# One PSUM pool for a whole network: rings turned by hand in place of a pool opened anew

## The chip, the cores and the metric

The kernel runs on one core of a Trainium2 chip. Its time is device microseconds (us) of one execution, from three executions of the kernel before: 2588.32, 2590.48 and 2588.38 us, median 2588.38 us. A fourth execution was profiled; it took 2587.3 us. A core has five engines[...]: TensorE (PE, matmuls), VectorE (DVE), ScalarE (ACT), GpSimd (POOL) and SyncE (SP, which issues DMAs here). TensorE writes its results into PSUM, eight banks of 128 x 512 float32 values; VectorE and ScalarE read them there.

## The reference

A small network of four residual layers on an input of 4 images, each 512 channels by 32 x 32 positions, so T = 1024 tokens. Each layer normalizes its input by groups of channels and adds its result to it.

```python
x = x + L0(gn(x))   # attention, 8 heads: scores mixed across heads, softmax,
                    # instance norm of the whole map, values, projection
x = x + L1(gn(x))   # channel gate: means -> 9-qubit circuit -> linear -> sigmoid
x = x + L2(gn(x))   # plain attention, 8 heads of 64: q, k, v, softmax, values, projection
x = x + L3(gn(x))   # memory: scores against 2048 items, top 8, softmax, weighted sum of 8 rows
```

Layers 2 and 3 are the ones that the change touches, with the end of layer 0. In layer 2 each head computes `softmax(q^T k / 8) v` over 1024 x 1024 scores; in layer 3 each token takes the 8 best of 2048 rows:

```python
q, k, v = conv(x, Wq), conv(x, Wk), conv(x, Wv)
out = conv(einsum(softmax(einsum(q, k) * SCALE), v), Wp)           # layer 2
att = tokens @ mempool.T                                             # layer 3
vals, idx = top_k(att, 8); out = softmax(vals) weighted rows mempool[idx]
```

## The kernel before

All arithmetic is float32. The program is one long list of instructions, traced by `fast_net` image by image; a second version, `general_net`, stands behind a branch that the inputs here never take. A scheduler orders the instructions of each engine; those wrapped in `pin(...)` keep the order in which they were written. The scheduler also places the semaphore waits: an instruction that overwrites a buffer waits for its last readers.

PSUM is used in two ways. For layer 0, a pool `ps_a` is opened at the top and gives out five fixed buffers: three pairs of banks, `pairs[0..2]` (each 128 x 2 x 512), and two single banks, `pv_bank` and `pt_bank`. The code names them itself: `project(..., at, ...)` takes `pairs[at % 3]` through `place` (L176). At L1434 to L1439 this pool is closed and two pools are opened in the same memory for layers 2 and 3: `ps_s` with three slots of two banks (tag `sc`) and `ps_m` with two slots of one bank (tag `mm`). From there a tile is asked for by `ps_s.tile(...)`, and the pool decides which slot it gets: the one that came free first in the order in which the scheduler placed the instructions.

The work around the change, in order of time:

- **End of layer 0, last image** (L1383 to L1432). The last steps of the attention run together with `take_q2`, the q projection of layer 2 for image 0 (`qs`, L1404). Then follow four k projections `ks[m](m + 1)` (L1413), the instance norm of the last image, four v projections `take_v2(0, i, i + 2)` (L1430, matmuls in L204), and four output projections `put_out(b, m, m)` (L1432, matmuls in L745). Each fills one pair of banks. q is taken out of PSUM by VectorE (L989), k by ScalarE (L996), v by VectorE (L1005). `put_out` ends in two VectorE additions per pair (L684), each followed by statistics (L699).
- **Layer 2** (L1458 to L1494). `UNITS2` cuts an image for one image into 16 units: 4 pairs of heads x 2 halves of the queries x 2 groups of four key blocks. `scores2` (L1009) computes four score tiles for a unit (L1027, two matmuls each into one pair of banks), and ScalarE takes their exponentials (L1021) into one of six places in SBUF. `apply2` (L1050) multiplies the exponentials of the unit before with v (L1064, eight matmuls into one `mm` bank). Of the four exponentials of a unit, two are issued before `apply2` and two inside it, after its first and second key block, because their place in SBUF is read by those matmuls. At every second unit `invert2` (L1084) sums the softmax denominators with two small matmuls (L1095) into an `sc` slot, which ScalarE copies out (L1099). POOL and VectorE add up exponentials for these sums (L1041, L1045, L1046, L1080, L1081). Small matmuls of the gate and the norms (`small_ps`, L1441) also take an `sc` slot for a moment.
- **Between images** the q, k and v projections of the next image and the output projection of this one run back to back (`place(None, ...)`, a slot of `ps_s`).
- **Layer 3** (L1515 to L1543): `attention` (L1170) fills two `sc` tiles per block of 128 tokens, `pick` finds the top 8 and gathers their rows, `read` and `read_last` transpose or sum the result through a `mm` bank (L1234, L1254).

Of the kernel before, what the change touches and what calls it, by code (L numbers as in the profile page):

```python
# [10 lines left out]
F32 = mybir.dt.float32  # L11
# [3 lines left out]
PSUM = bass.MemoryType.PSUM  # L15

P = 128
B = 4
C = 512
T = 1024  # L20
KC = C // P
TC = T // P
NB = 512
# [18 lines left out]
def fast_net(ctx: ExitStack, tc: tile.TileContext, a: dict, out: bass.AP, flag: bass.AP):  # L42
# [6 lines left out]
    stage = ctx.enter_context(ExitStack())  # L49
# [125 lines left out]

    def place(at, name):  # L176

        return pairs[at % 3] if at is not None else ps_s.tile([P, 2, NB], F32, tag="sc", name=name)

    def flat2(ps):  # L180
        return ps.rearrange("p n q -> p (n q)")
# [827 lines left out]
    def scores2(b, u, before=None):  # L1009

        m, n, t0 = u
        I = img[b]
        nm = f"c{b}_{m}_{n}"
        es, scs = [], []

        def exp2():
            e = places2[:, count[0] % 6]
            count[0] += 1  # L1020
            pin(nc.scalar.activation(e, scs[len(es)], AF.Exp))  # L1021
            es.append(e)

        for i, t in enumerate(range(t0, t0 + 4)):
            sc = ps_s.tile([P, 2, NB], F32, tag="sc", name=f"sc_{nm}_{t}")
            for r in range(2):
                pin(nc.tensor.matmul(  # L1027
                    sc[:, r, :],
                    I["k"][r * HD:(r + 1) * HD, m, t * P:(t + 1) * P],
                    I["q"][r * HD:(r + 1) * HD, m, n * NB:(n + 1) * NB],  # L1030
                    start=True, stop=True,
                ))
            scs.append(sc)
            if before is None or i < 2:
                exp2()
        if before is not None:
            apply2(b, before, exp2)
        I["e", u] = list(es)
        if t0 == 0:
            I["es", m, n] = sums2[:, (2 * m + n) % 2]  # L1040
            nc.gpsimd.tensor_add(I["es", m, n], es[0], es[1])  # L1041
            es = es[2:]
        for i in range(0, len(es), 2):
            two = pair_sum[:, (t0 + i) // 2 % 2]
            nc.gpsimd.tensor_add(two, es[i], es[i + 1])  # L1045
            nc.vector.tensor_add(I["es", m, n], I["es", m, n], two)  # L1046
        if t0 == TC - 4:
            over_keys(b, m, n)

    def apply2(b, u, exp2=None):  # L1050

        m, n, t0 = u
        I = img[b]
        if t0 == 0:
            invert2(b)
            I["pv", m, n] = ps_m.tile([P, NB], F32, tag="mm", name=f"pv_c{b}_{m}_{n}")
        else:
            finish2(b)
        pv = I["pv", m, n]
        for i, e in enumerate(I.pop(("e", u))):  # L1060
            t = t0 + i
            for r in range(2):
                h = 2 * m + r
                pin(nc.tensor.matmul(  # L1064
                    pv[r * HD:(r + 1) * HD, :], I["v"][:, t, h * HD:(h + 1) * HD],
                    e[:, r, :], start=(t == 0), stop=(t == TC - 1),
                ))
            if exp2 and i < 2:
                exp2()
        if t0 == TC - 4:  # L1070
            I["due"] = (m, n)
# [12 lines left out]
    def invert2(b):  # L1084

        I = img[b]
        due = I.pop("due", None)
        if due is None:
            return
        m, n = I["ready"] = due  # L1090
        nm = f"{b}_{m}_{n}"
        ps = ps_s.tile([P, 2, NB], F32, tag="sc", name=f"rs_{nm}")[:, 0, 0:NS]
        s_ = I.pop(("s", m, n)).rearrange("p r q -> p (r q)")
        for half in range(2):
            pin(nc.tensor.matmul(  # L1095
                ps[half * HD:(half + 1) * HD], same[:, half * HD:(half + 1) * HD], s_,
                start=True, stop=True))
        ri = small.tile([P, NS], F32, tag="ri", name=f"ri_c{nm}")
        nc.scalar.copy(ri, ps)  # L1099
        nc.vector.reciprocal(ri, ri)  # L1100
        ris = small.tile([P, NS], F32, tag="ssq", name=f"ris_{nm}")
        nc.vector.transpose(ris, ri)
        for bound, op in ((R_LO, ALU.is_ge), (R_HI, ALU.is_le)):
            nc.vector.scalar_tensor_tensor(seen0, ri, bound, seen0, op, ALU.add)
        rows = r_rows[n % 2]
        nc.sync.dma_start(out=rows, in_=ris[0:NS])
        rb = I["rb", m, n] = apool.tile([P, NB], F32, tag="rb", bufs=2, name=f"rb_c{nm}")
        for r in range(2):
            nc.sync.dma_start(
                out=rb[r * HD:(r + 1) * HD],  # L1110
                in_=rows.rearrange("(r q) x -> r (q x)", r=2)[r].partition_broadcast(HD))
# [58 lines left out]
    def attention(b, tt, between=None):  # L1170

        nm = f"{b}_{tt}"
        att = eight_k([P, NI], f"att_{nm}")
        for i, (lo, hi) in enumerate(
                ((0, T), (T, T + NB), (T + NB, NI)) if (b, tt) == tiles[-1] else ((0, T), (T, NI))):
            sc = ps_s.tile([P, T], F32, tag="sc", name=f"at_{nm}_{i}")
            for i0 in range(lo, hi, NB):
                for k in range(KC):
                    pin(nc.tensor.matmul(  # L1179
                        sc[:, i0 - lo:i0 - lo + NB],  # L1180
                        xn3[b][:, k, tt * P:(tt + 1) * P], memT[k][:, i0:i0 + NB],
                        start=(k == 0), stop=(k == KC - 1),
                    ))
            pin(nc.scalar.copy(att[:, lo:hi], sc[:, 0:hi - lo]))  # L1184
            if between is not None and i == 0:
                between()
        return att
# [43 lines left out]
    def read_last(b, tt, picked, dg):  # L1231

        got, et, rs, xr = picked
        tp = ps_m.tile([P, KC, P], F32, tag="mm", name=f"stp_{b}_{tt}")  # L1234
        for i in range(TOPK):
            for m in range(KC):
                pin(nc.tensor.matmul(
                    tp[:, m, :], got[:, i, m * P:(m + 1) * P], dg[:, i, :],
                    start=(i == 0 and m == 0), stop=(i == TOPK - 1),
                    skip_group_check=True,  # L1240
                ))
        return tp, xr

    def read(b, tt, picked):
        got, et, rs, xr = picked
        nm = f"{b}_{tt}"
        weigh(et, rs, nm)
        acc = apool.tile([P, NB], F32, tag="rb", bufs=2, name=f"acc_{nm}")
        pin(nc.vector.tensor_scalar_mul(acc, got[:, 0, :], et[:, 0:1]))
        for i in range(1, TOPK):  # L1250
            pin(nc.vector.scalar_tensor_tensor(  # L1251
                acc, got[:, i, :], et[:, i:i + 1], acc, ALU.mult, ALU.add
            ))
        tp = ps_m.tile([P, KC, P], F32, tag="mm", name=f"stp_{nm}")  # L1254
        for m in range(KC):
            pin(nc.tensor.transpose(tp[:, m, :], acc[:, m * P:(m + 1) * P], ident))
        return tp, xr
# [126 lines left out]
    for b in range(B):  # L1384
# [25 lines left out]
            collect_last(b)  # L1410
        load, take = statistics(b + 2) if b + 2 < B else (None, None)
        for m in range(KC):
            ks[m](m + 1)  # L1413
            next(state["behind"], None)
            for at in range(2 * m, 2 * m + 2):
                if load and m > 0:
                    take(at - 2)
                if load:
                    load(at)
# [3 lines left out]
        if last:  # L1423
            run_out(instance_norm(b))
            for n in range(KC):
                norm_quarter(b, n)
            bv2 = apool.tile([P, C], F32, tag="o2", name="bv2")
            nc.sync.dma_start(out=bv2, in_=a["bv"].partition_broadcast(P))
            for i in range(TC // 2):
                take_v2(0, i, i + 2)  # L1430
            for m in range(KC):
                put_out(b, m, m)  # L1432

    stage.close()  # L1434
    pairs.clear()
    by_scalar.append(True)
    stage = ctx.enter_context(ExitStack())
    ps_s = stage.enter_context(tc.tile_pool(name="ps_s2", bufs=3, space=PSUM))
    ps_m = stage.enter_context(tc.tile_pool(name="ps_m2", bufs=2, space=PSUM))  # L1439

    def small_ps(name):  # L1441
        return ps_s.tile([P, 2 * NB], F32, tag="sc", name=name)

    places2 = eT_flat[:, 0:6 * 2 * NB].rearrange("p (i r q) -> p i r q", i=6, r=2)
    sums2 = eT_flat[:, 6 * 2 * NB:8 * 2 * NB].rearrange("p (i r q) -> p i r q", i=2, r=2)
# [50 lines left out]
    def check_range():  # L1496

        tot = small.tile([P, 1], F32, tag="tot", name="tot")
        nc.vector.tensor_reduce(tot, seen0, AX.X, ALU.add)
        tps = ps_m.tile([P, NB], F32, tag="mm", name="tot")  # L1500
        nc.tensor.matmul(tps[:, 0:1], ones, tot, start=True, stop=True)
        nc.vector.tensor_scalar(
            flag, tps[0:1, 0:1], float(2 * P * NS * B * (TC + 2 * KC)), None, ALU.not_equal)
# [745 lines left out]
```

## Time and profile before

| | before |
|---|---|
| median of three runs | 2588.38 us (2588.32 to 2590.48) |
| profiled execution | 2587.3 us, span 2585.5 us |
| PE busy | 2533.4 us (98%), idle 47.3 us inside the span |
| ACT, DVE, POOL busy | 986.9, 1548.0, 1199.9 us |
| layer 0 | 0 to 1268.5 us |
| layer 2 | 1270.8 to 2123.1 us |
| granted TensorE clock | 0.999 of full speed |

The span runs from the first to the last instruction; 1.8 us of the profiled execution's time lie outside of it. PE is the engine to watch: it is busy nearly everywhere, so time can be won only where it idles, and is lost where it begins to wait. In the lines shown below, a timeline row has the start in us, the duration, the engine, the line of the program, the operation with what it writes and reads, and in square brackets how long the engine had stood idle before it and what ended that. A row of the waits has the waiter, what it waited for, the total in us, how often, and the longest.

### The profile page before, as it was taken

How to read it: one execution, taken by the hardware profiler on the slowest of the kernel's cores; microseconds unless marked ns; L12 is line 12 of the kernel's file. 1: busy time of each engine (PE TensorE's matmuls, PEld its weight loads, DVE VectorE, ACT ScalarE, POOL GpSimd, SP SyncE). 2: the span in 40 equal slices, each digit the busy share in tenths (PEclk: the TensorE clock that was granted, in tenths of full speed). 3: DMA queues.
4: the chain of work that ended last, by engine and by line, in shares of the span. 5: the costliest groups of instructions: out<-in, count | busy, mean ns of one | idle time of the engine just before them, and what ended most of it. 6: DMA issues, size and time to landing. Idle time of an engine off the chain costs nothing.

```text
span 2585.5 us, 47491 instructions
## 1 busy us (share of the span) xinstructions
PE 2533.4 (98%) x18438; PEld 1162.9 (45%) x18438; DVE 1548.0 (60%) x2668; ACT 986.9 (38%) x1165; POOL 1199.9 (46%) x1700
## 2 busy tenths in 40 slices
PE   8999999999999999999999999999999999999998
PEld 3344535544355534555533433443343344444445
DVE  4599348872788338881466047225614647878876
ACT  1467236651666236651252145125304622121211
POOL 3266415543455425553284047017404616656565
PEclk9999999999999999999999999999999999999999
DMA  2578448872698439883300120030012036667666
GB/s 82 144 208 233 124 125 228 232 205 82 180 239 235 113 95 224 236 254 122 130 18 15 68 101 21 25 137 27 13 42 97 22 110 184 216 185 219 180 192 180
DMA packets 186969, 358.22 MB, mean 139 GB/s; under 512 B 32873, under 2 KB 96361, under 8 KB 183026
## 3 DMA queue, kind: packets, MB, share of 16 engines
q1 hardware_dynamic: 105504, 175.57, 21.9%
q0 software_dynamic: 49152, 142.79, 20.1%
q10 hardware_dynamic: 32082, 36.76, 5.1%
q8 instruction: 148, 2.42, 0.4%
q14 instruction: 83, 0.68, 0.1%
HBM read 186.96 MB, written 33.82 MB: 85 GB/s over the span
## 4 chain that ended last, share of the span: by engine, by line
PE 74%; issue 8%; POOL 7%; DMA 7%; ACT 2%; DVE 1%; SPq 0%; POOLq 0%; ACTq 0%; DVEq 0%
PE pair L192 10%; PE sc_c L1027 9%; PE pv_c L1064 9%; PE pv L532 8%; POOL got L1204 7%; PE pair L467 6%; PE pair L493 5%; PE pt L425 4%; PE pt L721 4%; PE p L192 3%; PE k L192 3%; PE q L192 3%; PE v L204 3%; DMA got<-in_mem,ix 3%; DMA s<-ss 3%
## 5 line engine op out<-in xcount | busy, mean ns | idle before, releaser
L482 POOL DMA_DIRECT2D s<-ss x512 | 258.2, 511 | 399.1 <-ACT ss L473 103.3
L506 DVE STREAM_TRANSPOSE eT<-e 128x1024 f32<-128x1024 f32 x256 | 316.8, 1238 | 195.4 <-ACT e L500 194.9
L1204 POOL DMA_INDIRECT got<-in_mem,ix x256 | 277.6, 1085 | 216.2 <-DVE tmx L1210 144.3
L1021 ACT ACTIVATE eT<-sc_c 128x1024 f32<-128x1024 f32 x256 | 247.9, 1022 | 289.2 <-PE sc_c L1027 210.4
L521 DVE BATCH_NORM_STATS2 st<-e 128x6 f32<-128x256 f32 x1024 | 351.1, 406 | 0.0
L500 ACT ACTIVATE e<-pair 128x1024 f32<-128x1024 f32 x256 | 250.4, 1022 | 168.7 <-PE pair L493 139.0
L1045 POOL TENSOR_TENSOR e<-eT 128x1024 f32<-128x1024 f32 x96 | 235.6, 2457 | 161.6 <-ACT eT L1021 100.5
L467 PE MATMUL pair<-k,q 64*32 64x512 f32 x4096 | 267.1, 598 | 12.7 <-ACT e L500 12.7
L473 ACT COPY ss<-pair 128x1024 f32<-128x1024 f32 x256 | 247.2, 1020 | 78.6 <-PE pair L467 37.5
L532 PE MATMUL pv<-eT,v 128*64 128x128 f32 x4096 | 250.7, 276 | 8.9 <-ACT pv L592 8.9
L532 PEld LDWEIGHTS pv<-eT,v 128*64 128x64 f32 x4096 | 221.1, 137 | 76.7 <-issue 54.5
L1046 DVE TENSOR_TENSOR eT<-eT,e 128x1024 f32<-128x1024 f32 x96 | 138.7, 1444 | 179.0 <-POOL e L1045 178.9
L1027 PE MATMUL sc_c<-q,k 64*128 64x512 f32 x1024 | 237.2, 602 | 2.4 <-DVE xr L684 2.3
L1064 PE MATMUL pv_c<-eT,v 128*64 128x512 f32 x1024 | 234.7, 601 | 1.6 <-DVE eT L1121 1.6
L1041 POOL TENSOR_TENSOR eT<-eT 128x1024 f32<-128x1024 f32 x32 | 80.0, 2500 | 335.8 <-ACT eT L1021 332.0
L493 PE MATMUL pair<-s,wmix 32*32 32x512 f32 x4096 | 161.8, 599 | 3.1 <-DMA s<-ss 1.9
L1251 DVE SCALAR_TENSOR_TENSOR acc<-got,et,acc 128x512 f32<-128x512 f32 x210 | 157.9, 752 | 7.5
L1027 PEld LDWEIGHTS sc_c<-q,k 64*128 64x128 f32 x1024 | 93.5, 186 | 131.7 <-issue 72.0
L1184 ACT COPY att<-at 128x1024 f32<-128x1024 f32 (+1 forms) x65 | 64.9, 999 | 220.9 <-PE at L1179 220.8
L467 PEld LDWEIGHTS pair<-k,q 64*32 64x32 f32 x4096 | 57.1, 105 | 179.6 <-ACT e L500 86.3
L1064 PEld LDWEIGHTS pv_c<-eT,v 128*64 128x64 f32 x1024 | 68.4, 138 | 139.9 <-issue 138.1
L1179 PE MATMUL at<-memT,xn_d 128*128 128x512 f32 x256 | 120.7, 594 | 0.0
(295 smaller groups left out, 3299.4 us busy)
## 6 DMA issues: line engine op xcount, KB each, us to landing
s<-ss SPq DMA_DIRECT2D x512, 128.0 KB
s<-ss POOLq DMA_DIRECT2D x512, 128.0 KB, 4.6
rb<-r POOLq DMA_DIRECT2D x64, 128.0 KB, 6.1
o<-o SPq DMA_DIRECT2D x32, 256.0 KB
xr<-in_x ACTq DMA_DIRECT2D x32, 256.0 KB
x<-xr SPq DMA_DIRECT2D x32, 256.0 KB
xr_c<-x SPq DMA_DIRECT2D x32, 256.0 KB
rb_c<-r SPq DMA_DIRECT2D x64, 128.0 KB
```

The costliest lines, as they stand in the source:

```text
L192: pin(nc.tensor.matmul(ps[:, n, :], w[:, k, m * P:(m + 1) * P], rhs(k, n), start=(k == 0), stop=(k == KC - 1),))
L467: pin(nc.tensor.matmul(sc[m * NS:(m + 1) * NS, r, :], q[r * HD:(r + 1) * HD, m, s * NS:(s + 1) * NS], k_[r * HD:(r + 1) * HD, m, n * NB:(n ...
L482: pin(relays[side].dma_start(out=s2[2 * m + r::NH], in_=ss[m * NS:(m + 1) * NS, r, :]))
L493: pin(nc.tensor.matmul(mixed(s, r // 2)[t * NS:(t + 1) * NS, r % 2, :].rearrange("p (qq k) -> p qq k", qq=2), wmix[r * NS:(r + 1) * NS], s ...
L500: pin(nc.scalar.activation(e[:, half].rearrange("p r qq k -> p (r qq k)"), flat2(mixed(s, half)), AF.Exp))
L506: pin(nc.vector.transpose(eT[:, j % 2].rearrange("p b (qq i r) x -> p i r qq b x", qq=2, i=4)[:, i, 2 * half:2 * half + 2], e[:, half].rea ...
L521: pin(nc.vector.bn_stats(st[:, i, 2 * half + r, qq, :], e[:, half, r, qq, :]))
L532: pin(nc.tensor.matmul(pv[r * HD:(r + 1) * HD, gp, :], I["v"][:, t, g * HD:(g + 1) * HD], eT[:, j % 2, t, :, 4 * g:4 * g + 4], start=(t == ...
L1021: pin(nc.scalar.activation(e, scs[len(es)], AF.Exp))
L1027: pin(nc.tensor.matmul(sc[:, r, :], I["k"][r * HD:(r + 1) * HD, m, t * P:(t + 1) * P], I["q"][r * HD:(r + 1) * HD, m, n * NB:(n + 1) * NB] ...
L1064: pin(nc.tensor.matmul(pv[r * HD:(r + 1) * HD, :], I["v"][:, t, h * HD:(h + 1) * HD], e[:, r, :], start=(t == 0), stop=(t == TC - 1),))
L1204: pin(nc.gpsimd.indirect_dma_start(out=got[:, i, :], out_offset=None, in_=a["mem"], in_offset=bass.IndirectOffsetOnAxis(ap=ix[:, i:i + 1], ...
```

## The change

The pool of layer 0 is no longer closed. Its three pairs and two banks serve layers 2 and 3 through two counters: `next_pair` hands out pairs 0, 1, 2, 0, ... and `next_bank` alternates between `pt_bank` and `pv_bank`, in the order in which the program is written. Every `ps_s.tile` becomes `next_pair()`, every `ps_m.tile` becomes `next_bank()`. The projections at the end of layer 0 use other pairs: k takes 2, 0, 1, 2 (before 1, 2, 0, 1), v takes 1, 2, 0, 1 (before 2, 0, 1, 2), and the output projection takes 2, 0, 1, 2 (before 0, 1, 2, 0).

```diff
@@ place
-        return pairs[at % 3] if at is not None else ps_s.tile([P, 2, NB], F32, tag="sc", name=name)
+        return pairs[at % 3] if at is not None else next_pair()
@@ scores2
         for i, t in enumerate(range(t0, t0 + 4)):
-            sc = ps_s.tile([P, 2, NB], F32, tag="sc", name=f"sc_{nm}_{t}")
+            sc = next_pair()
@@ apply2
-            I["pv", m, n] = ps_m.tile([P, NB], F32, tag="mm", name=f"pv_c{b}_{m}_{n}")
+            I["pv", m, n] = next_bank()
@@ invert2
-        ps = ps_s.tile([P, 2, NB], F32, tag="sc", name=f"rs_{nm}")[:, 0, 0:NS]
+        ps = next_pair()[:, 0, 0:NS]
@@ attention
-            sc = ps_s.tile([P, T], F32, tag="sc", name=f"at_{nm}_{i}")
+            sc = flat2(next_pair())
@@ read_last
-        tp = ps_m.tile([P, KC, P], F32, tag="mm", name=f"stp_{b}_{tt}")
+        tp = next_bank().rearrange("p (k q) -> p k q", q=P)
@@ read
-        tp = ps_m.tile([P, KC, P], F32, tag="mm", name=f"stp_{nm}")
+        tp = next_bank().rearrange("p (k q) -> p k q", q=P)
@@ end of layer 0
         for m in range(KC):
-            ks[m](m + 1)
+            ks[m](m + 1 + last)
...
             for i in range(TC // 2):
-                take_v2(0, i, i + 2)
+                take_v2(0, i, i + 1)
             for m in range(KC):
-                put_out(b, m, m)
-
-    stage.close()
-    pairs.clear()
+                put_out(b, m, m + 2)
+
     by_scalar.append(True)
-    stage = ctx.enter_context(ExitStack())
-    ps_s = stage.enter_context(tc.tile_pool(name="ps_s2", bufs=3, space=PSUM))
-    ps_m = stage.enter_context(tc.tile_pool(name="ps_m2", bufs=2, space=PSUM))
+    turns = [0, 0]
+
+    def next_pair():
+        turns[0] += 1
+        return pairs[(turns[0] - 1) % 3]
+
+    def next_bank():
+        turns[1] += 1
+        return (pv_bank, pt_bank)[turns[1] % 2]
 
     def small_ps(name):
-        return ps_s.tile([P, 2 * NB], F32, tag="sc", name=name)
+        return flat2(next_pair())
@@ check_range
-        tps = ps_m.tile([P, NB], F32, tag="mm", name="tot")
+        tps = next_bank()
```

A line that starts with `@@` names the function or place that the lines stand in. In the built program of the changed kernel every engine has its instructions in the very order of before, the DMAs of SP, ACT and POOL included. What differs is which bank a matmul writes, and what 131 instructions wait for: 91 of PE, 22 of ACT and 18 of DVE.

## The prediction

> **What bounds the kernel now.** I read the page's head first, then the waits of PE, then the timeline around the places that the diff touches.
>
> ```profile
> span 2585.5 us, 47491 instructions
> PE 2533.4 (98%) x18438; PEld 1162.9 (45%) x18438; DVE 1548.0 (60%) x2668; ACT 986.9 (38%) x1165; POOL 1199.9 (46%) x1700
> ```
>
> PE is busy 98% of the span. A change that adds and removes no matmul can win only PE's idle time, and can lose by making PE idle. The waits of PE, longest first, say where it idles:
>
> ```profile
> PE pair L467 <- ACT e L500: 12.7, 57, 1.5
> PE pv L532 <- ACT pv L592: 8.9, 15, 1.6
> PE pt L145 <- DVE mv L313: 7.4, 1, 7.4
> PE stp L1237 <- DMA got<-in_mem,ix: 2.4, 4, 1.2
> PE sc_c L1027 <- DVE xr L684: 2.3, 1, 2.3
> PE rs L1095 <- DVE s_c L1081: 2.0, 1, 2.0
> ...
> PE pv_c L1064 <- DVE eT L1121: 1.6, 1, 1.6
> ```
>
> The first three are in layer 0 and its start, which keep their code. From the end of layer 0 to the end of the program PE idles, as far as this view shows, only in the other four rows, 8.3 us together, over 1300 us. One of them stands exactly at the border where one pool was closed and the next opened: 2.3 us, once. The timeline there:
>
> ```profile
> 1268.50 0.75 DVE L684 SCALAR_TENSOR_TENSOR xr<-pair,bproj,xr 128x512 f32<-128x512 f32 x1 [3.49 <-PE pair L745]
> 1269.29 0.69 DVE L699 BATCH_NORM_STATS2 st_b<-xr 128x6 f32<-128x512 f32 x1
> 1269.90 0.73 DVE L684 SCALAR_TENSOR_TENSOR xr<-pair,bproj,xr 128x512 f32<-128x512 f32 x1
> ...
> 1270.78 7.14 PE L1027 MATMUL sc_c<-q,k 64*128 64x512 f32 x32 [2.31 <-DVE xr L684]
> ...
> 1271.99 5.61 ACT L1021 ACTIVATE eT<-sc_c 128x1024 f32<-128x1024 f32 x6 [49.44 <-PE sc_c L1027]
> ```
>
> The last projection's matmuls end at 1268.46. VectorE takes the result out in two additions, the second ending at 1270.63. Only then does the first score matmul of layer 2 start, at 1270.78, though it writes other banks.
>
> [...]
>
> **Part 1: the border.** Before, the first score tile waits for the last addition, because the new pool's first tile waits for the old pool as a whole. After, it writes `pairs[0]`, which held output projection 1 (the second of four); its addition ended at 1258.29, 12.5 us ahead. The second tile writes `pairs[1]`, free since 1264.04. The third writes `pairs[2]`, and that is free at 1270.63 only. So:
>
> - Tile 0 starts at 1268.46 and takes 0.93 (as 1270.78 to 1271.71 before), tile 1 takes 0.86: until 1270.25.
> - Tile 2 starts 0.15 after the addition ends, as tile 0 did before: 1270.78. PE idles 0.53 there in place of 2.31: gain 1.78.
> - Tiles 2 to 7 then need 6 x 0.858 = 5.15: until 1275.93. Before, all eight ended at 1277.84, a little held back by ScalarE, which takes 0.92 for each of six exponentials in a row while PE needs 0.86 per tile. ScalarE now has a head start: exponential 4 ends near 1274.78, tile 7 is due at 1275.07, so it holds nothing back. Gain 1.91 in all when the first `pv_c` matmul starts.
>
> The first six exponentials and the first POOL addition come about 2.3 us earlier; later ones follow PE's matmuls again (at 1279.03 ScalarE waits for `pv_c`, at 1280.07 POOL waits for ScalarE), so everything downstream moves by 1.9 us.
>
> **Part 2: the other order of pairs in the last projections.** k starts on pairs 2 and 0, which q used in its last two projections; v starts on 1 and 2, which k used in its last two. So at four places only one projection (6.9 us of PE) lies between two uses of a pair in place of two. I find each evacuation in the trace: q 2 and q 3 leave PSUM by 1167.8 and 1176.9, the projections that reuse their pairs begin at 1182.6 and near 1190. k 2 is out at 1205.30 and v 0 starts at 1213.12 (7.8 to spare, before 15.4); k 3 is out at 1212.16, v 1 starts at 1220.07 (7.9 to spare). Cost 0; if these evacuations came 8 us later, each such us would be lost. The output projections keep two between. No DMA or instruction changes its place in any queue.
>
> **Part 3: the ring in layer 2.** This is where the change could lose. In 27 places a score tile or small tile follows `invert2`. The pool gave it the slot that ScalarE's copy of the denominators (L1099) had just freed, and that copy comes before the unit's last two exponentials on ScalarE. The ring gives it the next pair in writing order, which must wait for the third exponential, and the tile after it for the fourth. One such place:
>
> ```profile
> 1292.64 0.18 ACT L1099 COPY ri_c<-rs 128x32 f32<-128x32 f32 x1 [0.81 <-PE rs L1095]
> 1293.58 1.94 ACT L1021 ACTIVATE eT<-sc_c 128x1024 f32<-128x1024 f32 x2 [0.76 <-PE pv_c L1064]
> ...
> 1295.98 3.70 PE L1027 MATMUL sc_c<-q,k 64*128 64x512 f32 x16
> ```
>
> Old slack: 1295.98 - 1292.82 = 3.16. New slack: the first of the pair of exponentials ends at 1294.61, so 1.37 remain; the fourth ends at 1295.52 and the second tile starts at 1296.94, 1.42 remain. The same sums give 1.37 or more at all 27 first places. At 8 of them a small matmul stands between, and the tile after it has 0.77 to 0.94 left. How little is enough? Every fourth tile of a unit already reuses a pair that ScalarE freed 0.42 us before (61 of them at 0.4, smallest single case 0.05), and PE idles at none. So 0.77 is enough: cost 0. In return the third tile no longer waits for anything; it had 1.7 to 2.3 to spare, gain 0.
>
> **Part 4: the extra waits.** ACT gets 4 and DVE 14 more separate wait instructions (17 to 51 ns each in the trace), PE 3 fewer. The new ones wait for a reader of the same banks for which PE itself had to wait before it wrote them, so they are over when reached. They lie on evacuations of q, k and v, one projection ahead of their users. At most 18 x 0.05 = 0.9 us on engines that are 38% and 60% busy, behind 6.9 us of PE each: 0. PE drops five waits on its own earlier matmuls (before 1270.78, 2081.2, and three in layer 3); PE idles at none but the first, so 0.
>
> **The sum.** The profiled execution: span 2585.5 - 1.9 = 2583.6, time 2587.3 - 1.9 = 2585.4. The median of the three runs lies 1.1 above the profiled one; 2588.38 - 1.91 = 2586.5 us. That is 0.07% of the whole, less than the 0.2% (5.2 us) that about marks what a measurement of this kernel can tell from no change.
>
> **Where it could go otherwise.** Between the border and the end stands one stall of some size:
>
> ```profile
> 1369.24 1.24 DVE L1081 TENSOR_REDUCE s_c<-est 128x16 f32<-128x512 f32 x2
> ...
> 1370.62 0.31 PE L1095 MATMUL rs<-s_c,same 128*64 128x32 f32 x4 [2.03 <-DVE s_c L1081]
> ...
> 1372.58 5.35 PE L1064 MATMUL pv_c<-eT,v 128*64 128x512 f32 x16 [1.64 <-DVE eT L1121]
> ```
>
> There VectorE is late behind POOL (the gate's small steps and the additions of exponentials). [...]L1046 takes 1.22 alone and 3.4 beside POOL. POOL last waited for ScalarE 14 us ahead (1356.28), so this stall should move along with PE.
>
> - **Rival 1, the gain is swallowed:** VectorE and POOL do not move along, and the stall at 1370 grows by what PE won. For it: lengths of L1046 depend on chance overlaps. Against: POOL's wait for ScalarE at 1356.28. Time 2588.4. Chance 0.13.
> - **Rival 2, the stall goes too:** with POOL ahead by some tenths, the overlaps fall otherwise and the 3.67 us vanish. 2588.38 - 1.91 - 3.67 = 2582.8, the only way to more than 0.2%. Chance 0.07.
> - **Rival 3, slower:** the ring binds. If ScalarE's third exponential comes later than the slack of 1.37 (or the fourth than 0.77), PE waits in each of 27 places. It decides against the gain from 1.91 / 27 = 0.07 us per place on, and against 0.2% from (5.2 + 1.9) / 27 = 0.26 per place, which would put the time at 2593.6. For it: the wait is later by 1.8 us in all 27 places. Against: 61 waits with 0.42 cost nothing. Chance 0.06.
> - **Rival 4, the change does nothing:** some other wait holds the first score tile at 1270.78. Against: all else it needs, q and k, was out of PSUM by 1212.2. Chance 0.04, time 2588.4, counted with rival 1.
>
> **How the numbers follow.** My forecast, 1.9 us faster with nothing else moved, has 0.70; rivals 1 and 4 have 0.17, rival 2 0.07, rival 3 0.06. So faster by over 0.2%: 0.07; slower: 0.06; within: 0.87. The range reaches from between rival 2 and the forecast up past rival 1, with the spread of the runs shown (2.2 us upward): 2583.6 to 2589.6.
>
> **What would show it.** Right: the waits of PE have no 2.3 us of L1027 on L684, but one of about 0.5, at the third score tile; the first score matmul starts right after L745; the first `pv_c` comes 1.9 us earlier; no new row of L1027 on ACT L1021. Wrong: new idle time of PE before L1027, L145, L886 or L901 with ACT L1021 as what ended it (rival 3), or rows of L1095 and L1064 on VectorE of more, or less, than 3.7 us (rivals 1 and 2).

## The result and the profile after

The changed kernel takes 2581.53 us in the median of 19 executions (2578.68 to 2584.81); the kernel before, run beside it, 2588.38 us (2581.82 to 2592.83, also 19). The ratio is 0.9979, with a 95% interval of 0.9972 to 0.9985. The time lies below the predicted range of 2583.6 to 2589.6.

Single executions spread by some 2 to 3 us, so sums are made below from means, with the standard error behind. Over all runs of this study the kernel before has a mean of 2586.1 +- 0.2 (196 executions), the changed kernel 2581.5 +- 0.3 (40). The median of the three executions that the prediction started from, 2588.38 us, lies 2.3 us above that mean.

The head of the profile after, and the waits of PE in it, those in layers 2 and 3 and the longest of layer 0:

```profile
span 2578.1 us, 47506 instructions
PE 2529.9 (98%) x18438; PEld 1161.5 (45%) x18438; DVE 1550.2 (60%) x2668; ACT 987.2 (38%) x1165; POOL 1200.4 (47%) x1700
PE pair L467 <- ACT e L500: 12.8, 57, 1.5
PE pv L532 <- ACT pv L592: 8.9, 15, 1.6
PE pt L145 <- DVE mv L313: 7.3, 1, 7.3
PE pt L1237 <- DMA got<-in_mem,ix: 1.7, 2, 1.0
PE pt L1064 <- DVE eT L1121: 1.5, 1, 1.5
...
PE pv L1064 <- DVE eT L1121: 0.3, 1, 0.3
...
PE pair L1027 <- DVE xr L684: 0.3, 1, 0.3
```

The longest waits of layer 0 are those of before. The 2.3 us of L1027 on L684 are 0.3. The row of L1095 on L1081 (2.0 us) is gone altogether; L1064 on L1121 is left with 1.5 us (1.6 before) and has a new 0.3. PE's idle time falls from 47.3 to 43.4 us. But PE is also 3.5 us less busy (2533.4 to 2529.9), with as many matmuls, so some matmuls ran faster. Of these 3.5 us, 1.1 lie in the first 145 us of the program, where nothing was changed (the clock record reaches full speed at 15.3 us in place of 17.5), and about 1.7 in a stretch shown below. The border, in the timeline after:

```profile
1263.66 2.32 PE L745 MATMUL pair<-eT 128*128 128x256 f32 x10
1265.91 1.99 PE L1027 MATMUL pair<-q,k 64*128 64x512 f32 x8
...
1267.41 0.73 DVE L684 SCALAR_TENSOR_TENSOR xr<-pair,bproj,xr 128x512 f32<-128x512 f32 x1
...
1268.20 4.13 PE L1027 MATMUL pair<-q,k 64*128 64x512 f32 x18 [0.31 <-DVE xr L684]
...
1273.56 2.79 PE L1064 MATMUL pt<-eT,v 128*64 128x512 f32 x12
```

The score matmuls now begin directly behind the last projection's, eight of them (two tiles) before PE waits for the last addition. The last projection ends at 1265.98 here. The first score tile starts 0.07 us ahead of that end (the rows overlap a little), where before it started 2.32 us behind it: 2.39 us gained. Up to the first matmul of L1064, 0.59 is given back, most of it at the third tile. That matmul comes 7.58 us after the last projection in place of 9.38 (1268.46 to 1277.84): a gain of 1.80 us, where 1.91 was forecast.

The second gain lies a hundred microseconds later, where the code is the same. In the timeline before, these are the rows that matter ahead of the stall at 1370 and that the prediction did not show:

```profile
1358.91 2.17 ACT L1021 ACTIVATE eT<-sc_c 128x1024 f32<-128x1024 f32 x2 [0.97 <-PE sc_c L1027]
...
1361.31 3.65 PE L1064 MATMUL pv_c<-eT,v 128*64 128x512 f32 x16
...
1362.49 1.94 ACT L1021 ACTIVATE eT<-sc_c 128x1024 f32<-128x1024 f32 x2 [1.42 <-PE pv_c L1064]
...
1364.51 2.38 POOL L1045 TENSOR_TENSOR e<-eT 128x1024 f32<-128x1024 f32 x1
1364.60 3.38 DVE L1046 TENSOR_TENSOR eT<-eT,e 128x1024 f32<-128x1024 f32 x1
```

And the same place in the timeline after:

```profile
1354.62 1.94 ACT L1021 ACTIVATE eT<-pair 128x1024 f32<-128x1024 f32 x2 [0.97 <-PE pair L1027]
...
1357.02 3.65 PE L1064 MATMUL pv<-eT,v 128*64 128x512 f32 x16
...
1358.48 1.94 ACT L1021 ACTIVATE eT<-pair 128x1024 f32<-128x1024 f32 x2 [1.93 <-PE pv L1064]
...
1360.25 1.22 DVE L1046 TENSOR_TENSOR eT<-eT,e 128x1024 f32<-128x1024 f32 x1
...
1360.50 3.19 POOL L1045 TENSOR_TENSOR e<-eT 128x1024 f32<-128x1024 f32 x1 [0.45 <-ACT eT L1021]
...
1362.73 1.24 DVE L1081 TENSOR_REDUCE s_c<-est 128x16 f32<-128x512 f32 x2
...
1364.23 0.31 PE L1095 MATMUL pair<-s_c,same 128*64 128x32 f32 x4
...
1366.06 3.65 PE L1064 MATMUL pt<-eT,v 128*64 128x512 f32 x16 [1.52 <-DVE eT L1121]
```

Before, POOL's addition begins 0.09 us ahead of VectorE's, and VectorE's takes 3.38 us. After, VectorE is ahead by 0.25 us; its addition takes 1.22 and POOL's is the long one (3.19 in place of 2.38). L1081, which PE's L1095 waits for, is then two microseconds earlier relative to PE, and no wait is left. About 0.5 us of this is given back at 1381, where the new wait of 0.33 us for L1121 stands. In both profiles the one that begins second is the slow one; why it is slowed was not shown.

The faster matmuls are in the view of windows, whose last three columns are the granted TensorE clock, the share of the DMAs and GB/s. First before, the sixteen `pv_c` matmuls behind the stall; then after, a window on their counterparts:

```profile
1372.58:1377.93 5.35, 5.35 (x18) 1.53 (x18) 5.35 (x4) 2.05 (x2) 3.30 (x2) 0.68 0.00 0
```

```profile
1366.00:1370.00 4.00, 3.94 (x18) 1.36 (x20) 4.00 (x4) 1.94 (x2) 2.71 (x1) 1.00 0.00 0
```

Behind the two idles of 2.03 and 1.64 us TensorE ran at a clock of 0.68 over the window: four pairs of matmuls came every 0.85 us in place of every 0.43, and from 1372.62 to 1376.03 us the clock was 0.50. Behind the single idle of 1.52 us it was 1.00. So the stall costs its idle time, less what remains, plus the slow matmuls: 2.03 + 1.64 - 1.52 + 4 x 0.42 = 3.8 us.

### The profile page after: what moved, and what is told of

Its sections match the earlier page's. It is cut to its first block, busy times and chain, and to the rows that moved or that the text cites. A ratio compares the mean times of both kernels' runs of the same rounds, so it can differ in the third digit from the quotient of the medians.

```text
span 2578.1 us, 47506 instructions
## 1 busy us (share of the span) xinstructions
PE 2529.9 (98%) x18438; PEld 1161.5 (45%) x18438; DVE 1550.2 (60%) x2668; ACT 987.2 (38%) x1165; POOL 1200.4 (47%) x1700
## 4 chain that ended last, share of the span: by engine, by line
PE 74%; issue 10%; POOL 8%; DMA 3%; ACT 3%; DVE 2%; SPq 0%; POOLq 0%; ACTq 0%; DVEq 0%
PE pair L192 21%; PE pv L532 8%; PE pair L1027 8%; POOL got L1204 7%; PE pair L467 6%; PE pair L493 6%; PE pt L425 5%; PE pair L204 4%; PE pv L1064 4%; PE pt L1064 4%; PE pt L721 4%; ACT e L500 2%; DMA s<-ss 2%; PE pair L1179 2%; PE pair L745 1%
## 5 line engine op out<-in xcount | busy, mean ns | idle before, releaser
L1021 ACT ACTIVATE eT<-pair 128x1024 f32<-128x1024 f32 x256 | 247.8, 1022 | 286.6 <-PE pair L1027 209.8
L1045 POOL TENSOR_TENSOR e<-eT 128x1024 f32<-128x1024 f32 x96 | 234.9, 2450 | 160.6 <-ACT eT L1021 125.9
L1046 DVE TENSOR_TENSOR eT<-eT,e 128x1024 f32<-128x1024 f32 x96 | 138.7, 1444 | 173.3 <-POOL e L1045 173.2
L1027 PE MATMUL pair<-q,k 64*128 64x512 f32 x1024 | 237.5, 602 | 0.6 <-DVE xr L684 0.3
L1041 POOL TENSOR_TENSOR eT<-eT 128x1024 f32<-128x1024 f32 x32 | 78.8, 2463 | 332.8 <-ACT eT L1021 329.0
L1027 PEld LDWEIGHTS pair<-q,k 64*128 64x128 f32 x1024 | 93.2, 186 | 130.4 <-issue 72.4
L1184 ACT COPY att<-pair 128x1024 f32<-128x1024 f32 (+1 forms) x65 | 64.9, 999 | 221.2 <-PE pair L1179 221.0
L1179 PE MATMUL pair<-memT,xn_d 128*128 128x512 f32 x256 | 120.7, 594 | 0.0
L1179 PE MATMUL pair<-memT,eT 128*128 128x512 f32 x256 | 120.4, 593 | 0.0
L1179 PE MATMUL pair<-eT 128*128 128x512 f32 x256 | 120.3, 592 | 0.0
```

The lines of the kernel that those rows point to most:

```text
L1027: pin(nc.tensor.matmul(sc[:, r, :], I["k"][r * HD:(r + 1) * HD, m, t * P:(t + 1) * P], I["q"][r * HD:(r + 1) * HD, m, n * NB:(n + 1) * NB] ...
L1179: pin(nc.tensor.matmul(sc[:, i0 - lo:i0 - lo + NB], xn3[b][:, k, tt * P:(tt + 1) * P], memT[k][:, i0:i0 + NB], start=(k == 0), stop=(k == ...
```

## The experiments

**Theory.** The border gives about what was worked out. The rest comes from the race above: whichever of POOL's L1045 and VectorE's L1046 begins first decides whether the stall is there. **Rivals.** The ring's banks or waits remove the stall; or the order of pairs gains by itself; or the earlier border shifts everything so that the stall falls away. The start of both engines can be counted from the first of the sixteen matmuls L1064 of that step, at 1361.31 before and 1357.02 after.

### The new order of pairs alone

The kernel before, its pools kept:

```diff
-            ks[m](m + 1)
+            ks[m](m + 1 + last)
...
-                take_v2(0, i, i + 2)
+                take_v2(0, i, i + 1)
...
-                put_out(b, m, m)
+                put_out(b, m, m + 2)
```

> The kernel before with one part of the change alone: the pools stay as they were, the last projections take the pairs in the new order. Theory (the order itself is worth nothing, and the stall of PE at 1370 us hangs on which of VectorE and POOL begins its addition first there): the wait of 2.3 us at the border stays, no projection waits; the stall either stays whole (time within 0.5 us of before) or is gone whole (3.4 to 3.9 us less), since ScalarE has one instruction less ahead of that place than before. Rival (the other order frees banks earlier and is a part of the gain by itself): 1 to 2 us less at the border or in the projections.

Mean 2587.6 +- 0.6, ratio to before 1.0006 (0.9999 to 1.0013): the order gains nothing by itself. The border's wait is 2.3 us as before. The one profiled execution, at 2582.68 us, has no stall, though, and shows how narrow the race is:

```profile
1362.71 3.45 POOL L1045 TENSOR_TENSOR e<-eT 128x1024 f32<-128x1024 f32 x1 [0.19 <-ACT eT L1021]
1362.71 1.22 DVE L1046 TENSOR_TENSOR eT<-eT,e 128x1024 f32<-128x1024 f32 x1
```

Both begin in the same hundredth, and VectorE happened to be first. The mean, no lower than that of before, suggests that most executions of this kernel do have the stall; no trace shows it. One profile is one draw.

### The ring with the old order of pairs

The changed kernel, with the three lines above turned back.

> The changed kernel with the old order of pairs in the last k, v and output projections; the ring stays. The first score tile then takes the pair that the very last output projection used, so it must wait for its last addition again. Theory: the border has its wait of about 2.3 us back (1.7 us more than the changed kernel); the stall at 1370 us is not tied to the pairs, so if it stays away the time lies 3.4 to 4 us under the kernel before, and if it comes back, at the time of the kernel before. Rival (ring and order gain only together, 5.8 us or nothing): time of the kernel before, with the stall back because the border is back.

Mean 2584.7 +- 0.8, ratio 0.9993 (0.9983 to 1.0002): 2.2 +- 0.9 us less than before in the runs beside it, where 3.4 to 4 were expected without the stall, and by the ratio not told apart from before. The waits of PE in its profile:

```profile
PE pair L1027 <- DVE xr L684: 2.2, 1, 2.2
...
PE pt L1064 <- DVE eT L1121: 1.5, 1, 1.5
```

The border's wait is back and, in this execution, the stall is not: VectorE was ahead by 0.03 us. So the border's wait does not by itself bring the stall, and the border's gain needs ring and order together, since under the old order the first tile takes the pair emptied last.

### VectorE put first by hand, before and after

One line in each kernel. POOL then writes the half of its buffer that VectorE's L1046 is still reading, and so must wait for it, in this one unit:

```diff
-            two = pair_sum[:, (t0 + i) // 2 % 2]
+            two = pair_sum[:, 1 if (b, u) == (0, (3, 0, 0)) else (t0 + i) // 2 % 2]
```

> The kernel before, one line edited: in unit (3, 0, 0) of image 0 POOL's addition (L1045) writes the other half of its buffer, which VectorE's addition of the unit before (L1046) is just reading, so POOL must let VectorE go first at 1364.5 us. No other instruction and no bank changes. Theory (the stall is decided by which of the two begins first): L1046 there takes 1.2 us in place of 3.38, L1081 comes 2 us earlier, the wait of 2.03 us before L1095 goes and the 16 matmuls after the next wait take 3.6 us in place of 5.35: 3.4 to 3.9 us less than before. Rival (the stall hangs on the ring or on the banks): the stall stays, within 0.5 us of before, or more where POOL's delay costs.

Mean 2584.0 +- 0.4, ratio 0.9987 (0.9981 to 0.9994), from before's 2586.9 +- 0.3 in the runs beside it. With no bank and no wait of PE edited, the kernel before lost its stall:

```profile
1364.44 1.22 DVE L1046 TENSOR_TENSOR eT<-eT,e 128x1024 f32<-128x1024 f32 x1
...
1365.80 2.36 POOL L1045 TENSOR_TENSOR e<-eT 128x1024 f32<-128x1024 f32 x1 [1.56 <-DVE eT L1046]
...
1368.52 0.31 PE L1095 MATMUL rs<-s_c,same 128*64 128x32 f32 x4
```

That is the theory's sign and place. The size, 2.9 +- 0.6 us, is less than the 3.4 to 3.9 expected, which would fit a stall that occurs in only a part of before's executions. (A second set of runs, below, gives 1.1 +- 0.9.)

> The same one line in the changed kernel, where VectorE is first anyway in the profiled execution. Theory: nothing to gain in an execution where VectorE is first already, so 5.8 us less than before again, and a narrower spread if the order of the two varies from run to run in the changed kernel. Rival (the wait that the line adds for POOL is late elsewhere): 0.5 us or more slower than the changed kernel.

Mean 2582.0 +- 0.6, 4.9 us less than before, where 5.8 were expected; the changed kernel's own mean, from other sets of runs, is 2581.5. Nothing gained, as expected; a narrower spread (expected if its race varied) was not seen. In the changed kernel VectorE wins the race without help.

### VectorE made late in the changed kernel

```diff
             nc.gpsimd.tensor_add(two, es[i], es[i + 1])
+            if (b, u, i) == (0, (2, 1, 4), 2):
+                nc.vector.tensor_scalar_mul(two[:, 0], two[:, 0], 1.0)
             nc.vector.tensor_add(I["es", m, n], I["es", m, n], two)
```

> The changed kernel with one small VectorE instruction more (a product by 1.0 of 128x512 values of the addend itself) just before the addition L1046 that begins at 1360.25 in the changed kernel. It costs some 0.4 us of VectorE, which by itself is no cost to PE (PE waits 0.0 at 1364.2 there). The profiled runs so far put VectorE's start 3.14 to 3.30 us after the first matmul L1064 of that step and POOL's, in the changed kernel, 3.48 after it; so POOL is first now. Theory (whoever begins first decides): L1046 takes 3.4 us in place of 1.2, the waits before L1095 and L1064 come back (2 to 2.4 and 1.6 us) and the sixteen matmuls after them take over 5 us: 3.4 to 4.3 us more than the changed kernel, so 1 to 2 us less than before (the border's gain stays). Rival (the ring's banks took the stall away, VectorE's start has no part in it): at most 0.4 us more than the changed kernel.

Mean 2586.4 +- 0.5, ratio to before 1.0004 (0.9997 to 1.0011); 5.0 +- 0.6 more than the changed kernel in its own sets of runs. The timeline (line numbers are two higher behind the inserted lines):

```profile
1367.28 0.42 DVE L1047 TENSOR_SCALAR e<-e 128x512 f32<-128x512 f32 x1
...
1367.59 2.35 POOL L1045 TENSOR_TENSOR e<-eT 128x1024 f32<-128x1024 f32 x1 [0.50 <-ACT eT L1021]
...
1367.73 3.28 DVE L1048 TENSOR_TENSOR eT<-eT,e 128x1024 f32<-128x1024 f32 x1
...
1373.66 0.31 PE L1097 MATMUL pair<-s_c,same 128*64 128x32 f32 x4 [2.27 <-DVE s_c L1083]
...
1375.61 4.29 PE L1066 MATMUL pt<-eT,v 128*64 128x512 f32 x12 [1.64 <-DVE eT L1123]
```

An instruction of 0.42 us, on an engine 60% busy, brings the whole stall back: both waits and the slow matmuls. The ring is in place here, and the border's gain too, so the rival that the ring removes the stall falls. In the trace it costs 2.27 + 0.12 + 4 x 0.42 = 4.1 us; the mean lies above that by 1.5 standard errors.

### Why POOL is later in the changed kernel

The timelines above give it. POOL starts 0.08 us after a pair of ScalarE's exponentials is out, in both profiles. That is 3.20 us after the first matmul in the kernel before and 3.48 us in the changed one. ScalarE itself starts that pair of exponentials 1.18 us after the matmul before, 1.46 after (idle 1.93 in place of 1.42), while the pair ahead of it takes 2.17 us before and 1.94 after. So one instruction begins about 0.3 us late in both, but not the same one. Counted in ScalarE's records from the start of the trace, it is the 1728th in both. Up to there the changed kernel has two records less on ScalarE, both of them separate wait instructions (the order of pairs alone, and the ring alone, each take away one), and so the 1728th has become the exponential that POOL waits for. Two runs move that count.

Two copies more on ScalarE in the changed kernel, behind the output projections of layer 0:

```diff
                 put_out(b, m, m + 2)
+            idle = const.tile([P, KC], F32, tag="idle", name="idle")
+            for _ in range(2):
+                pin(nc.scalar.copy(idle, bq2))
```

> The changed kernel with two tiny ScalarE copies (128x4 values) more after the last output projection of layer 0, where ScalarE idles. In the traces one ScalarE instruction, always the same place in its stream counted from the program's start, begins 0.3 us late: in the kernel before it is the exponential ahead of the one that releases POOL, in the changed kernel, whose ScalarE stream is two instructions shorter up to there, it is the very one that releases POOL. The two copies put the count back to that of before. Theory (this lateness is what makes POOL second in the changed kernel): the late instruction is the exponential ahead again, POOL starts 3.20 us after the first matmul in place of 3.48, level with VectorE, and the stall comes back in a part of the executions: 1 to 4 us more than the changed kernel, its profile with POOL's start at 3.20. Rival (the shift of 7 us or the ring itself took the stall away): time of the changed kernel, POOL's start at 3.48.

```profile
1356.99 2.16 ACT L1021 ACTIVATE eT<-pair 128x1024 f32<-128x1024 f32 x2 [0.97 <-PE pair L1027]
...
1359.38 3.65 PE L1064 MATMUL pv<-eT,v 128*64 128x512 f32 x16
...
1360.57 1.94 ACT L1021 ACTIVATE eT<-pair 128x1024 f32<-128x1024 f32 x2 [1.42 <-PE pv L1064]
...
1362.53 1.22 DVE L1046 TENSOR_TENSOR eT<-eT,e 128x1024 f32<-128x1024 f32 x1
1362.59 3.38 POOL L1045 TENSOR_TENSOR e<-eT 128x1024 f32<-128x1024 f32 x1 [0.26 <-ACT eT L1021]
```

The 2.16 and the 1.42 are back, and POOL starts 3.21 us after the matmul, 0.06 behind VectorE. In this execution VectorE was still first. By the mean, 2583.9 +- 1.0, the kernel is 2.4 +- 1.1 slower than the changed one in its own sets of runs, with executions from 2577.8 to 2591.7, as a race would give that falls either way. The ratio to before is 0.9998 (0.9988 to 1.0009).

And the mirror, two instructions less on ScalarE in the kernel before:

```diff
-    nc.scalar.dma_start(out=gamma, in_=a["in_gamma"].partition_broadcast(P))
+    nc.gpsimd.dma_start(out=gamma, in_=a["in_gamma"].partition_broadcast(P))
...
-    nc.scalar.dma_start(out=beta, in_=a["in_beta"].partition_broadcast(P))
+    nc.gpsimd.dma_start(out=beta, in_=a["in_beta"].partition_broadcast(P))
```

> The mirror: the kernel before with two instructions less on ScalarE, both at the program's start (the loads of gamma and beta are issued by POOL in place of ScalarE); no bank, wait or order changes near the border or the stall. Theory: the late ScalarE instruction is now the exponential that releases POOL, POOL starts some 3.48 us after the first matmul in place of 3.20, VectorE is first in every execution, the stall is gone: about 2.9 us less than before by the mean (as with VectorE put first by hand, 2584.0), border wait of 2.3 us unchanged. Rival: time of before.

```profile
1364.43 3.65 PE L1064 MATMUL pv_c<-eT,v 128*64 128x512 f32 x16
...
1365.90 1.94 ACT L1021 ACTIVATE eT<-sc_c 128x1024 f32<-128x1024 f32 x2 [1.93 <-PE pv_c L1064]
...
1367.58 1.22 DVE L1046 TENSOR_TENSOR eT<-eT,e 128x1024 f32<-128x1024 f32 x1
...
1367.92 3.12 POOL L1045 TENSOR_TENSOR e<-eT 128x1024 f32<-128x1024 f32 x1 [0.53 <-ACT eT L1021]
```

Two loads issued by another engine 1350 us earlier, and POOL starts at 3.49 in place of 3.20, VectorE first by 0.34 us, the stall gone (the border's wait is 2.8 us in this execution). The time, 2583.9 +- 0.8, is where the theory puts it (2584.0), but the kernel before was at 2585.2 +- 0.4 in the runs beside it, and the ratio 0.9997 (0.9989 to 1.0005) doesn't tell the two apart. Here the trace carries the verdict, not the time.

### The parts side by side

> The changed kernel as it is, beside the next three on one chip, so that the parts can be summed from runs made side by side. 5 to 6 us less than before, about as the first time (2581.5 by the mean).

2581.5 +- 0.4, ratio 0.9985 (0.9978 to 0.9991), before at 2585.5 +- 0.4. The changed kernel repeats its time to the tenth; the gain is 4.0 us where 5 to 6 were expected, because before came out lower here.

The ring with the old order of pairs, and VectorE put first by the line above:

> The ring with the old order of pairs and VectorE put first at the place of the stall. Beside the twelfth run (the pools of before, the same line) it tells what the ring costs or gives by itself in layers 2 and 3, without the border's wait (both have it) and without the stall (neither has it). Theory and prediction: 0, within 0.7 us of each other, both near 2584.0. Rival (the 27 later waits or the 18 extra ones cost a little each): 0.05 us or more at each of 27 places would be 1.4 us or more.

The same line in the kernel before, a second time:

> The kernel before with VectorE put first, again, as the partner of the eleventh run. Near 2584.0, about 2 to 2.5 us over the changed kernel: the border's wait of 2.3 us and what half-rate matmuls follow it in some executions.

They have 2583.7 +- 0.7 (ratio to before 0.9993, 0.9985 to 1.0001) and 2584.4 +- 0.8 (0.9994, 0.9985 to 1.0003). So VectorE put first gains 1.1 +- 0.9 us here, where the first set gave 2.9 +- 0.6: this set alone does not tell it from nothing. The ring alone changes the time by -0.7 +- 1.1 us, and no row of L1027 on ScalarE's L1021 appears in the waits of any profile with the ring. A cost of 1.4 us or more for the 27 later waits lies at the very edge of what these times allow, and the waits show none of it. The kernel before with VectorE first ran into slow matmuls behind the border's idle, at a clock of 0.61:

```profile
1271.60:1276.00 4.40, 4.31 (x12) 2.17 (x14) 1.12 (x4) 1.68 (x2) 0.00 (x0) 0.61 0.87 307
```

Five profiles with 2.2 or 2.3 us of idle at the border show the clock behind it: it fell in three (this one, and 0.87 over 1262 to 1275 us both in the first run of the ring with the old order and in the first of the kernel before with VectorE first) and not in two (1.00 over the same window, before and with the new order alone). In two with the 0.3 us wait in its place, the changed kernel and the same with VectorE first, it was 1.00. At half clock for 3.41 us, as behind the stall, such a stretch costs about 1.7 us. So the border is worth about 1.80 + 3/5 x 1.7 = 2.8 us in the mean, an estimate from seven profiles. The times agree: the kernel before with VectorE first, both sets together, 2584.1 +- 0.4, less the changed kernel, 2581.5 +- 0.3, is 2.7 +- 0.5.

### A better version?

In the changed kernel PE still waits 1.5 us at 1366 for L1121, which stands on VectorE behind two normalizations of the next image (L975). This moves them a step back, with VectorE first by the line above:

```diff
-            for _ in range(2):
+            for i in range(2):
                 if s >= 3:
                     next(behind, None)
-                if s >= 8:
+                if s >= 8 and (b, s) != (0, 11) and (b, s, i) not in ((0, 13, 1), (0, 14, 1)):
                     next(ahead, None)
```

> A try at a better version: the changed kernel with VectorE put first at 1360 us (the line of the fourth run) and, for image 0, two of the four normalizations L975 of the next image's input moved by a step, behind the addition of the output L1121 that PE waits 1.5 us for at 1366 (the other two go one to each of the two following steps). L1121 then waits only for its factors, which land about 6 us after they were sent, near 1364.1, in place of 1365.33. Expected: 1.2 us less than the fourth run, 7 us less than before. It is nothing, or worse, if the later normalizations push the next such product (at 1380 us, where VectorE idles 1.9 us) past its time.

> The better version a second time, beside the changed kernel. Its profile has no wait of 1.5 us before L1064 near 1366 and nothing in its place. Expected 1 to 1.5 us under the changed kernel by the mean; if the 0.9 us between the two so far was the difference of chips, 0.

```profile
1367.92 0.68 DVE L1121 TENSOR_TENSOR eT<-pt,rb_c 128x512 f32<-128x512 f32 x1
...
1368.66 3.65 PE L1064 MATMUL pt<-eT,v 128*64 128x512 f32 x16
```

The wait is gone in the first profile (0.3 us in the second), with nothing in its place. The times: 2580.6 +- 0.4 (ratio to before 0.9981, 0.9975 to 0.9988), then 2581.2 +- 0.9 (0.9986, 0.9977 to 0.9994). The second time it lies 0.3 us under the changed kernel beside it, where 1 to 1.5 were expected. Together 2580.8 +- 0.5 against 2581.5 +- 0.3 of the changed kernel. It beats the kernel before; that it beats the changed one is likely by the trace and not shown by the times.

## Why the prediction was wrong

**Bound and part 1: right, one term short.** 1.80 us in the pair of profiles against 1.91 worked out, and the wait at the third tile that was named (0.31 and not 0.53). What the sum lacked is that an idle of 2.3 us can cost a second time, in matmuls at half clock behind it (24 of L1027 took 6.99 us in place of 5.42 in the first run of the kernel before with VectorE first); so it is not only PE's idle time that can be won. The profile before had no such stretch at the border (clock 1.00 over 1262 to 1275 us), but it had one behind the stall at 1370, in plain sight: `x16` in 5.35 us in a row that the prediction quoted. The means put the border at 0.75 +- 0.5 us over the 1.91; the half clock explains that in size, and no run separates it.

**Parts 2 to 4: right as costs.** No cost of the other order, of the 27 later waits of the ring or of the extra wait instructions is seen: the order alone has ratio 1.0006, the ring alone -0.7 +- 1.1 us, and there is no new wait on ScalarE's exponentials. Rivals 1, 3 and 4 did not happen. But part 4 priced the wait instructions by their own length only. Ahead of the stall ScalarE has two fewer, not more, and that their number moves a late record onto another exponential was put at nothing.

**"Where it could go otherwise": the step that failed.** It said that POOL "last waited for ScalarE 14 us ahead (1356.28), so this stall should move along with PE". That was read from the idle times in the timeline, which show only waits in which the engine stood still. POOL's L1045 at 1364.51 shows no idle, but ScalarE's pair of exponentials had ended at 1364.43, 0.08 us ahead: POOL was tied to ScalarE there. VectorE began 0.20 us after POOL's addition before that one (L1041) had ended, in both profiles; in the kernel before that was 0.09 us behind POOL's start. The stall hung on that difference, and the changed kernel's ScalarE stream, two wait instructions shorter, puts POOL 0.28 us later.

**Rival 2 is what happened,** given a chance of 0.07 and 3.67 us. Its cause was right in kind ("the overlaps fall otherwise"), wrong in that POOL is later and not ahead; its price left out the slow matmuls and the 1.5 us that stay. The stall costs 3.8 us where it occurs (some 3.3 after what is given back at 1381). In the mean it is worth 2586.1 - 2584.1 = 2.0 +- 0.5 us, so by estimate the kernel before has it in half of its executions or somewhat more. Its one profile shows the stall; how many executions have it was not seen.

**The miss, summed.** Predicted 2586.5, measured 2581.5 in the mean over all runs: 2.29 us because the start lay above the mean of before (2588.38 and 2586.09), 1.96 for the stall (2586.09 - 2584.13), and 0.75 at the border (2584.13 - 2581.47 - 1.91), which is what remains and which the half clock would explain. The last two are uncertain by about 0.5 each, and the first by how the level of the kernel before differed between sets of runs: beside the result it was 2587.8 +- 0.7, so that the gain was 6.3 us there and 4.0 in the last set.

What stays open: why ScalarE's record of that number is late (the last section has what the traces say of it), and why the mean of the kernel before differed from one set of runs to the next (2585.2 to 2587.8), whether by the share of executions with the stall or otherwise.

## What to carry to other kernels

Where a VectorE and a POOL addition like L1046 and L1045 come due within some tenths of a microsecond, compare both starts with the end of what each waited for, not with idle times: here the one that started second paid for it (0.8 us on POOL, 2.2 us on VectorE), and two instructions more or fewer on ScalarE, far ahead, moved POOL's start by about 0.28 us (3.48 to 3.21, 3.20 to 3.49). Price a stall of TensorE as its idle time and the slow matmuls behind it (3.8 us here, 1.7 of them the matmuls). Before a small gain is forecast, ask how far single executions of the kernel before lie apart, and whether the profiled one is typical.

## What the runs showed that was not expected

- **An instruction late by its number.** In the traces before and after, the 1728th record of ScalarE is an exponential that begins 0.33 us after its wait was over, and the 1856th one that is late by 0.32. The late exponential near the stall shows in eleven profiles: in four it is in the pair ahead of the one that POOL waits for (2.16 or 2.17 us for that pair in place of 1.94), in seven it is the first that POOL waits for (idle of 1.93 us). In the other three (the order alone, both with the ring and the old order) no exponential there is late (1.94 us and an idle of 1.64). Adding or taking two instructions far ahead moves it, as the two runs on the count showed (POOL's start at 3.21 in place of 3.48, and at 3.49 in place of 3.20). What makes these records late was not shown.
- **Half clock after short idles.** Matmuls at half clock followed the stall in the two profiles that have it: idles of 2.03 and 1.64 us before (clock 0.68 over the sixteen matmuls behind) and of 2.27 and 1.64 with VectorE made late (twelve matmuls in 4.29 us in place of 2.79). They followed the border's idle of 2.2 or 2.3 us in three of five profiles. In the first run of the kernel before with VectorE first the clock was also 0.65 over 1209.6 to 1214 us, in layer 0, about where L651 waits 0.9 us (the place is an estimate from L651 at 1212.88 in the profile before). But they followed none of ten idles of 1.4 to 1.6 us before L1064: the sixteen matmuls behind took 3.65 us in eight profiles, and the clock was 1.00 over 1362 to 1380 us in the other two. So the length of an idle alone doesn't decide it; what does was not shown. The stretch before lasted 3.41 us, so it cost some 1.7 us by estimate, and such stretches would make a part of the spread between executions.
